# A second split product for pairs of gate tiles, a split product at the start of the first block's down stage, and a fixed bank

## The chip, the cores and the metric

The kernel runs on one core of a Trainium2 chip. TensorE (PE) multiplies matrices into the eight PSUM banks; ScalarE (ACT) and VectorE (DVE) read and write PSUM and SBUF; GpSimd (POOL) works on SBUF alone; SyncE (SP) issues the DMAs. The metric is the device time of one execution in microseconds.

## The reference

The input x is 4 x 2048 tokens of 512 channels, all in fp32. The output is x plus an RWKV-4 attention and a gated feed-forward, both on the same layer norm of x:

```python
xn = layernorm(x)
r, k, v = (mu * xn + (1 - mu) * shifted) @ W.T            # for each of the three, 512 -> 512
attn = (sigmoid(r) * wkv(k, v, w, u)) @ Wo.T
hidden = silu(xn @ W1.T) * (xn @ W3.T)                    # 512 -> 2048
out = x + attn + fwht(hidden) @ W2.T                      # fwht: Hadamard transform, folded into W2
```

`wkv` is a recurrence over time for each channel. In the reference it keeps a running maximum; the kernel computes it with three scans on VectorE and exponentials and relus on ScalarE.

## The kernel before, in words

The tokens are worked on in eight **blocks** of 1024 (two for each batch entry). A block has three parts: the projections k, v and r (six pairs of 128-row tiles), the **up stage** (gate and linear part of the feed-forward, 16 **tiles** `j` = 0 to 15 of 128 hidden units) and the **down stage** (W2 and Wo together, on the 2048 hidden and 512 attention rows). Blocks repeat every 368.6 us in the steady state.

Matrix products are made by the seven-product form of a 2x2 block multiplication. For an up tile (`up_rest`) the four blocks are W1 and W3 over the two halves of the channels; the right side is the normalized input, halves of channels by halves of 512 tokens. Seven combinations of weights, **forms** 0 to 6, are kept in DRAM (`part_w`), and each is multiplied with one combination of the input: form 0 with `b11` (part of `xnT`), form 4 with the first sum `t1` (in `tf`). A form's product is two matmuls of 128x128 weights with 512 columns; in the trace an fp32 matmul leaves two records. Between products ScalarE copies a bank's partial result into another bank, and VectorE adds the stored product of form 4, called `s5`.

Form 0 is already split once more. Two tiles 2p and 2p+1 share their right side, so the form-0 weights of both tiles are again a 2x2 block, and `pair_product` makes seven matmuls with half as many columns (256) where four with 512 would stand. The text calls its steps **P0 to P6** by the number given to `matmul`; they come in the order P1, P0, P2, P4, P5, P3, P6. The pair's weights are made in block 0 by POOL (`make_pair`, `keep_pair`), are kept in `pair_w` and are loaded for each pair from block 1 on. The sums of the right side lie in `pair_sums` (in row 0 of `k_sb`, free by then). The result of a pair lands in `pair_out`, the left half by a ScalarE copy and the right half by a VectorE sum, and `fill` copies it into the banks `pb` and `pa` of each tile. Pairs begin with `FIRST_PAIR` = 2, so tiles 4 to 15 are filled this way: their products are forms 4, 5, 1, 3, 6 and 2, in this order, on the banks pf, pb, pa, pb, pc and pd. The product of pair p is computed beside tile 2p-2, one or two of its steps after each form.

The order on each engine is written out by hand: everything is issued through `InOrder` (line 36 in every row of the profile), and each engine works its queue in that order. `up_pairs` drives a tile as a generator and calls the pair's generator after each of its steps. `step()` issues one of the 40 **pieces** of the recurrence (`wkv`): in blocks from 1 on each of the four rows h has ten pieces, row 0 in the projections and rows 1 to 3 over five tiles each (tiles 1 to 5, 6 to 10, 11 to 15), two pieces per tile. Pieces 9 and 10 are the longest on VectorE (a half reciprocal, the numerator, the two final products); they fall on tiles 5, 10 and 15. Between the pieces VectorE does the gate of each tile: the sums with s5, `h0` and `h1`, and at the start of the next tile the **tail** (tanh of h1 on ScalarE, then h0 times pd, h1 times pc, h1 times pb).

Banks are handed out by `take` and given back by `give`, oldest first, from block 1 on; block 0 rotates with `bank()`. In the down stage the pieces of weights (five tiles of 128x128 each) stream through eight slots of `pieces_w`. Blocks 1 to 7 (`down`) split every form once more (`Deep`): seven steps of five 256-wide matmuls. Block 0 (`down_whole`) has plain products: four pieces of five 512-wide matmuls for each form. `Deep.clear` zeroes half a bank on ScalarE before the first step; `before` issues the tail of tile 15 and what is left of the recurrence. `Chores` spreads the next blocks' statistics and normalizing over the down stage, and `normalize_early` normalizes the block after next during the up stage, through slots in `pieces_w`.

Of the kernel before, what the change touches and what calls it, by code (L numbers as in the profile page):

```python
# [41 lines left out]
def tile_rwkv_attn_hadamard_ffn(  # L42
# [37 lines left out]
    down_w = dram.tile([2, 7, KH, P, QR, P], F32, name="down_w")  # L80
    deep_w = dram.tile([7, 7, P, QR, P], F32, name="deep_w")

    pair_w = dram.tile([NF // 2, P, 7, P], F32, name="pair_w")
    stat_d = dram.tile([n_blocks, 2, TB], F32, name="stat_d")
    xn_d = dram.tile([C, TB], F32, name="xn_d")

# [7 lines left out]
    sa, sb = (const.tile([P, OFF + TB], F32, name=n) for n in ("sa", "sb"))  # L94
    e1b, e1 = (const.tile([P, TB], F32, name=n) for n in ("e1b", "e1"))
    banks = [ps.tile([P, H], F32, name=f"bank{b}") for b in range(8)]
    free_banks = deque(banks)

    NP = NF // 2

# [22 lines left out]
    def take():  # L123
        return free_banks.popleft()
# [6 lines left out]
    tf_flat = tf.rearrange("p f k t -> p (f k t)")  # L131
    x_first, x_tok = (flat.rearrange("p (t c) -> p t c", c=C) for flat in (k_flat, tf_flat))

    pair_sums = k_sb[:, 0, :].rearrange("p (n t) -> p n t", n=4)
    pair_out = v_sb[:, 0, :].rearrange("p (n t) -> p n t", n=2)
    pair_s5 = unit(NF - 1)[:, 0 : H // 2]

    pair_forms = pieces_w[:, 7].rearrange("p q c -> p (q c)")[:, 0 : 4 * P].rearrange("p (f c) -> p f c", f=4)
    spread = v_sb[:, 0:2, :]
    stage = [v_sb[:, 2 + s // 2, ts(s % 2, H)] for s in range(4)]  # L140
    u2_of = [e1b[:, ts(g, H)] for g in range(KH)]
# [80 lines left out]
    def normalize_early(i):  # L222

        flat = pieces_w.rearrange("p u q c -> p (u q c)")
        both = flat[:, 0 : 2 * TB].rearrange("p (s t) -> p s t", t=TB)
        slots = [flat[:, ds((2 + n) * TB, TB)] for n in range(3)]

        def load(b):
            sp.dma_start(out=slots[b % 3], in_=xT[ts(b, P), ds(i * TB, TB)])

        load_spread(i, both)
        for b in range(3):
            load(b)
        yield
        for b in range(NB):
            xb = slots[b % 3]
            for s, op in ((0, ALU.mult), (1, ALU.add)):
                dve.tensor_tensor(xb, xb, both[:, s, :], op)
                if s:
                    sp.dma_start(out=xn_d[ts(b, P), :], in_=xb)  # L240
                    if b + 3 < NB:
                        load(b + 3)
                yield


# [226 lines left out]
    def load_parts(i, chunk):  # L472
        kind, n = chunk
        t = ring_a.tile([P, 7, KH, P], F32, tag="a", name=f"part_{i}_{kind}_{n}")
        if kind == "pair":
            sp.dma_start(out=t.rearrange("p f k c -> p (f k) c")[:, 0:7], in_=pair_w[n])
        elif kind == "rest":
            sp.dma_start(out=t[:, 1:7], in_=part_w[n][:, 1:7])
        elif is_first(i, n):
            sp.dma_start(out=t[:, 0:4], in_=wpart[n])  # L480
            forms_in(t)
        else:
            sp.dma_start(out=t, in_=part_w[n])
        return t

    def make_pair(p, w0, w1):
        (a11, a12), (a21, a22) = ([w[:, 0, b] for b in range(KH)] for w in (w0, w1))
        seven_forms([pair_forms[:, n] for n in range(4)], a11, a12, a22, a21)
        sp.dma_start(out=pair_w[p][:, 0:2], in_=w0[:, 0])
        sp.dma_start(out=pair_w[p][:, 2], in_=w1[:, 0, 1])  # L490

    def keep_pair(p):
        sp.dma_start(out=pair_w[p][:, 3:7], in_=pair_forms)

    def is_first(i, n):
        return i == (1 if n < 3 * KH else 0)
# [59 lines left out]

    def fill(row):

        pb, pa = take(), take()
        act.copy(pb, pair_out[:, row])
        act.copy(pa, pair_out[:, row])
        return pa, pb

    def up_rest(key, j, w, filled, tail, step, then):

        m11, m21, m22, f1, f2, f3, f4 = right_of["up"]
        h0, h1 = unit(j)[:, 0:H], unit(j)[:, H:TB]

        def product(pt, form, right, start=False):
            for b in range(KH):
                pe.matmul(
                    pt, lhsT=w[:, form, b, :], rhs=right[:, b, :], start=start and b == 0, stop=b == KH - 1,
                    skip_group_check=True,
                )

        if filled:
            pa, pb = filled
        else:  # L580
            pa, pb = take(), take()
            product(pa, 0, m11, True)
            act.copy(pb, pa)
        pf = take()
        product(pf, 4, f1, True)
        s5 = small.tile([P, H], F32, tag="s5", name=f"s5_{key}")
        act.copy(s5, pf)
        give(pf)
        yield
        product(pb, 5, f2)  # L590
        pc = take()
        act.copy(pc, pb)
        for f in tail:
            f()
        yield
        product(pa, 1, m21)
        act.activation(h0, pa, AF.Tanh, scale=0.5)
        yield
        product(pb, 3, f3)
        dve.scalar_tensor_tensor(h0, h0, 1.0, pa, ALU.add, ALU.mult)  # L600
        give(pa)
        pd = take()
        act.copy(pd, pb)
        yield
        step()
        dve.tensor_tensor(pb, pb, s5, ALU.add)
        product(pc, 6, m22)
        dve.tensor_tensor(pc, pc, s5, ALU.add)
        yield
        then()  # L610
        step()
        product(pd, 2, f4)
        yield (
            lambda: act.activation(h1, pc, AF.Tanh, scale=0.5),
            lambda: dve.tensor_tensor(h0, h0, pd, ALU.mult),
            lambda: dve.scalar_tensor_tensor(h1, h1, 1.0, pc, ALU.add, ALU.mult),
            lambda: dve.tensor_tensor(h1, h1, pb, ALU.mult),
            lambda: give(pd, pc, pb),
        )

    def pair_quarters():
        return [b11[:, b, cols] for b in range(KH) for cols in (lo, hi)]

    def make_pair_sums():
        q11, q12, q21, q22 = pair_quarters()
        t1, t2, t3, t4 = (pair_sums[:, n] for n in range(4))
        for out, x, y in ((t1, q12, q11), (t2, q22, t1), (t3, q22, q12), (t4, q21, t2)):
            difference(out, x, y)

    def pair_product(w):  # L630

        w = w.rearrange("p f k c -> p (f k) c")
        q11, _, q21, q22 = pair_quarters()
        t1, t2, t3, t4 = (pair_sums[:, n] for n in range(4))
        a, b = take(), take()

        def matmul(n, pt, right, start=False):
            pe.matmul(pt, lhsT=w[:, DEEP_AT[n]], rhs=right, start=start, stop=True, skip_group_check=True)

        def out(row, pt):  # L640
            act.copy(pair_out[:, row, lo], pt[:, lo])
            dve.tensor_tensor(pair_out[:, row, hi], pt[:, hi], pair_s5, ALU.add)


        matmul(1, a[:, hi], t1, True)
        act.copy(pair_s5, a[:, hi])
        yield
        matmul(0, a[:, lo], q11)
        act.copy(b[:, hi], a[:, lo])
# [8 lines left out]
        yield  # L658
        matmul(6, b[:, lo], t4)
        yield  # L660
        out(0, a)
        out(1, b)
        give(a, b)
        yield

# [1 line left out]

    def up_pairs(i, chunk, tail, step, beside):

        filled = None  # L670
        for j in range(1, NF):
            w = chunk(2 if j % 2 and j > 1 else 1)
            beside(j)
            ahead = []

            def fill_next():
                if 2 * FIRST_PAIR <= j + 1 < NF:
                    ahead.append(fill((j + 1) % 2))

            rest = up_rest(f"{i}_{j}", j, w, filled, tail, step, fill_next)  # L680
            product = iter(())
            for n in range(6):
                left = next(rest)
                if n == 0 and j % 2 == 0 and j + 2 < NF:
                    product = pair_product(chunk(0))
                next(product, None)
            tail, filled = left, ahead[0] if ahead else None
        return tail
# [85 lines left out]
        return [("deep", m, n) for n in which]  # L774

    order = (0, 1, 4, 6, 5, 3, 2)
    whole_program = [p for form in order for p in plain(form)]
    program = [p for n in (0, 4, 1, 2, 3, 5) for p in (*deep(6, n), *deep(0, n))]
    program += [*deep(1, 0), *deep(6, 6), *deep(0, 6)]
    for m, *which in (  # L780
# [75 lines left out]
                    self.product(("plain", form, (rh, g)), pts[g], rows, whole, start and rh == 0)  # L856
                then(g)

    def down_whole(i, chores, next_parts):

        d = Down(i)
        y11, y12, y21, y22 = (parts_of(kh, half) for kh in range(2) for half in range(2))
        pa, pb, pc = ([bank() for _ in range(KH)] for _ in range(3))
        s5 = [small.tile([P, H], F32, tag="s5", name=f"s5_{i}_d{g}") for g in range(KH)]
        d.residual(x11, 0, 0)
        d.plain_product(0, pa, (0, 0), lambda g: act.copy(pb[g], pa[g]), True)
        differences(y11, y12, y11)
        chores.start()
        chores.statistics(2 * TP + 1)
        next_parts()  # L870

        def c11(g):
            add(x11[g], pa[g])
            d.store(x11[g], 0, g, 0)

        d.plain_product(1, pa, (1, 0), c11)
        d.residual(x12, 0, 1)
        d.residual(x22, 1, 1)
        d.plain_product(4, pc, (0, 0), lambda g: act.copy(s5[g], pc[g]), True)
# [75 lines left out]
    def down(i, chores, next_parts, last, before):  # L955
# [1 line left out]
        d = Down(i)  # L957
        y11, y12, y21, y22 = (parts_of(kh, half) for kh in range(2) for half in range(2))
        early = list(free_banks)
        late = [pt for pt in banks if not any(pt is b for b in early)]  # L960
        pa, sets = early[0:2], [[early[2], early[4], early[3]], late]

        def slot(flat, n=0):
# [271 lines left out]
    for i in range(n_blocks):  # L1235
# [111 lines left out]


        if i:
            make_pair_sums()  # L1350
            tail = up_pairs(i, chunk, tail, step, lambda j: staging(i, j))
        for j in range(NF if i == 0 else 0):
            if j % 2 and j > 2 * FIRST_PAIR:
# [35 lines left out]
                loaded[0] = 2  # L1389

        if i == 0:
            before()
            down_whole(i, Chores(i + 1), next_parts)
        else:
            down(i, Chores(i + 1), next_parts, last, before)

# [52 lines left out]
```

## Time and profile before

| | us |
|---|---|
| median of 3 runs (3011.78 to 3013.1) | 3012.85 |
| profiled run, device time | 3011.08 |
| its span in the trace | 3009.3 |
| PE busy | 2993.2 |
| DVE busy | 2428.0 |
| ACT busy | 1266.0 |
| down stage of block 0, PE start to the next block's first matmul | 301.71 to 422.12 |
| down stage of block 3, PE start | 1055.80 |

The profile's page gives the busy time of each engine, the chain of work that ended last (followed back from the last instruction to whatever released each step), and the costliest groups of instructions. A row of the timeline gives the start, the length, the engine, the operation with out<-in, the shape and a count, and in brackets the idle time before it and who ended it. Since the kernel has one line for all instructions, rows are told apart by their tiles: `right<-right,bank` on DVE is the gate, `e`, `e1b`, `sa` and `sb` are the recurrence, `bank<-...,part_pair` is a pair's step, `v_sb<-bank` is a pair's output.

By stage, in block 3: between 950 and 1000 us (tiles 6 to 10) DVE is busy 41.49 of 50.00 us and ACT 28.69; between 1035.20 and 1055.80 (tiles 14 and 15) DVE is busy 20.30 of 20.60 us. Between 1066 and 1168 (down stage) DVE is busy 91.09 of 102.00 us. PE is busy in all of these.

### The profile page before, as it was taken

To read this page: it belongs to the slowest core of one execution; us is meant where nothing else is said; L and a number is where in the kernel's file an instruction comes from. 1 tells how busy PE (TensorE), PEld (TensorE's weight loads), DVE (VectorE), ACT (ScalarE), POOL (GpSimd) and SP (SyncE) were. 2 spreads that over 40 slices of the span, in tenths; PEclk is the share of its full clock that TensorE was granted. 3 is DMA by queue.
4 is the path that set the end of the run, shared out by engine and by line. 5 is a ranking of instruction groups with operands and counts; after the bars stand their busy time and mean duration, and the time that the engine had idled before them with its cause. 6 is when DMAs were issued, how large, how long until landed. Compare 5 with 4: busy or idle time off the path is not lost.

```text
span 3009.3 us, 26145 instructions
## 1 busy us (share of the span) xinstructions
PE 2993.2 (99%) x8954; PEld 1699.2 (56%) x8954; DVE 2428.0 (81%) x2637; ACT 1266.0 (42%) x2328; POOL 230.5 (8%) x220
## 2 busy tenths in 40 slices
PE   8999999999999999999999999999999999999999
PEld 3444444448644486445854558545585446844568
DVE  7688547789878897788977889778887788877887
ACT  4334134553345523554235542455425454144441
POOL 4264012220000000000000000000000000000000
PEclk9999999999999999999999999999999999999999
DMA  4266523666423374233633336332463324622244
GB/s 177 90 222 226 220 88 126 225 231 234 139 102 112 110 235 134 103 113 115 231 120 121 106 142 210 116 119 96 158 202 118 121 99 136 203 96 74 92 141 150
DMA packets 154979, 440.22 MB, mean 146 GB/s; under 512 B 16352, under 2 KB 36320, under 8 KB 152672
## 3 DMA queue, kind: packets, MB, share of 16 engines
q1 hardware_dynamic: 154560, 437.97, 42.6%
q8 instruction: 72, 1.18, 0.2%
q10 hardware_dynamic: 288, 0.59, 0.1%
q14 instruction: 59, 0.48, 0.0%
HBM read 363.01 MB, written 75.49 MB: 146 GB/s over the span
## 4 chain that ended last, share of the span: by engine, by line
PE 92%; DVE 7%; ACT 1%; DMA 0%; issue 0%; SPq 0%; DVEq 0%; ACTq 0%
PE bank L36 92%; DVE e1b L36 3%; DVE right L36 2%; DVE bank L36 1%; DVE e L36 1%; DVE v_sb L36 0%; ACT bank L36 0%; DMA xnT<-xT 0%; DVE sa L36 0%; ACT right L36 0%; DVE sb L36 0%; SPq L36 0%; DVE xnT L36 0%; DVE tf L36 0%; DVEq L1445 0%
## 5 line engine op out<-in xcount | busy, mean ns | idle before, releaser
L36 ACT COPY bank<-bank 128x512 f32<-128x512 f32 (+1 forms) x701 | 344.2, 491 | 999.1 <-PE bank L36 956.8
L36 PE MATMUL bank<-right,pieces_w 128*128 128x256 f32 (+1 forms) x2928 | 736.4, 409 | 2.9 <-ACT bank L36 2.9
L36 PEld LDWEIGHTS bank<-right,pieces_w 128*128 128x128 f32 x2928 | 555.1, 190 | 173.1 <-issue 99.2
L36 PE MATMUL bank<-tf,part_rest 128*128 128x512 f32 x1344 | 611.3, 592 | 1.6 <-ACT bank L36 1.6
L36 PEld LDWEIGHTS bank<-tf,part_rest 128*128 128x128 f32 x1344 | 255.1, 190 | 279.3 <-issue 248.3
L36 PE MATMUL bank<-right,part_full 128*128 128x512 f32 x840 | 369.6, 593 | 0.0
L36 DVE SCALAR_TENSOR_TENSOR right<-right,bank 128x512 f32<-128x512 f32 x256 | 175.1, 684 | 240.1 <-ACT right L36 239.4
L36 DVE TENSOR_TENSOR right<-right 128x1280 f32<-128x1280 f32 (+2 forms) x236 | 327.7, 1414 | 13.0 <-PE bank L36 12.0
L36 PE MATMUL bank<-tf,part_full 128*128 128x512 f32 x704 | 324.8, 592 | 0.0
L36 PE MATMUL bank<-xnT,part_rest 128*128 128x512 f32 x672 | 315.8, 592 | 0.0
L36 PEld LDWEIGHTS bank<-right,part_full 128*128 128x128 f32 x840 | 158.4, 190 | 203.2 <-issue 183.9
L36 ACT ACTIVATE right<-bank 128x512 f32<-128x512 f32 x308 | 184.1, 600 | 155.7 <-PE bank L36 110.2
L36 PE MATMUL bank<-xnT,part_full 128*128 128x512 f32 x528 | 248.1, 592 | 0.0
L36 PEld LDWEIGHTS bank<-tf,part_full 128*128 128x128 f32 x704 | 133.8, 190 | 159.4 <-issue 149.7
L36 DVE RECIPROCAL e1b<-e1b 128x512 f32<-128x512 f32 x64 | 213.9, 3343 | 0.0
L36 DVE TENSOR_TENSOR bank<-bank,s 128x512 f32<-128x512 f32 x256 | 168.2, 691 | 42.3 <-PE bank L36 29.8
L36 PEld LDWEIGHTS bank<-xnT,part_rest 128*128 128x128 f32 x672 | 127.7, 190 | 130.9 <-issue 117.2
L36 DVE TENSOR_TENSOR right<-right,bank 128x512 f32<-128x512 f32 x256 | 173.9, 679 | 6.5 <-PE bank L36 2.0
L36 PEld LDWEIGHTS bank<-xnT,part_full 128*128 128x128 f32 x528 | 100.3, 190 | 117.8 <-issue 113.3
L36 ACT COPY s<-bank 128x512 f32<-128x512 f32 x128 | 74.5, 582 | 214.0 <-PE bank L36 213.0
L36 PE MATMUL bank<-k_sb,pieces_w 128*128 128x256 f32 x630 | 146.3, 379 | 0.0
L36 DVE SCALAR_TENSOR_TENSOR right<-xnT,vec,right 128x1024 f32<-128x1024 f32 x92 | 121.9, 1355 | 21.3 <-ACT right L36 21.3
(137 smaller groups left out, 3160.3 us busy)
## 6 DMA issues: line engine op xcount, KB each, us to landing
pieces_w<-deep_w SPq DMA_DIRECT2D x343, 320.0 KB, 3.1
part_rest<-part_w SPq DMA_DIRECT2D x84, 768.0 KB, 4.3
part_full<-part_w SPq DMA_DIRECT2D x64, 896.0 KB, 4.6
part_w<-part_full SPq DMA_DIRECT2D x22, 896.0 KB, 6.7
part_pair<-pair_w SPq DMA_DIRECT2D x42, 448.0 KB, 4.1
pieces_w<-down_w SPq DMA_DIRECT2D x56, 320.0 KB, 4.7
deep_w<-pieces_w SPq DMA_DIRECT2D x7, 2240.0 KB, 8.6
tf<-x SPq DMA_DIRECT2D x7, 2048.0 KB, 7.9
```

The lines of the kernel that those rows point to most:

```text
L36: return self.tc.keep_in_program_order(issue(*args, **kwargs))
```

## The change

Five things are changed.

- **A second split product.** `make_pair` also makes the seven weights of form 4 of both tiles (POOL's sums go through `k_sb` row 0), and `pair_w` keeps two sets. In blocks 2 to 7, `up_pairs` starts a second `pair_product` beside the odd tile 2p-1, with weights loaded into `pair_w1` (a part of `pieces_w`) and right-hand sums made from `t1` at tile 2 (`make_pair_sums(1)`, kept in unit 14). Its two results go straight into the `s5` buffers of tiles 2p and 2p+1. `up_rest` then leaves out its own product of form 4 and the copy of it.
- **Slots.** `normalize_early` has two slots for its rows instead of three, which frees the place of `pair_w1`.
- **Block 0's down stage.** The first form is no longer a plain product but a `Deep` one, and the four plain pieces of form 1 stand between its steps, on banks of their own (`pc`). The tail is issued after the clearing of two banks. The statistics of the next block and the next weights are issued after both forms instead of after the first.
- **Clearing.** `down_whole` now calls `before` itself.
- **The bank.** `down` orders the three banks of its late set so that `pd` of tile 15 (`last_d`) is the one that is cleared after the tail.

```diff
-    pair_s5 = unit(NF - 1)[:, 0 : H // 2]
+    pair_sums = [t.rearrange("p (n t) -> p n t", n=4) for t in (k_sb[:, 0, :], unit(NF - 2))]
+    pair_s5 = [unit(NF - 1)[:, ts(n, H // 2)] for n in range(2)]
+    pair_w1 = pieces_w.rearrange("p u q c -> p (u q c)")[:, ds(4 * TB, 7 * P)].rearrange("p (f c) -> p f c", f=7)
...
     def make_pair(p, w0, w1):
+        for n, form in enumerate((0, 4)):
+            (a11, a12), (a21, a22) = ([w[:, form, b] for b in range(KH)] for w in (w0, w1))
+            seven_forms([pair_forms[n][:, m] for m in range(4)], a11, a12, a22, a21)
+            sp.dma_start(out=pair_w[n, p][:, 0:2], in_=w0[:, form])
+            sp.dma_start(out=pair_w[n, p][:, 2], in_=w1[:, form, 1])
...
-        pf = take()
-        product(pf, 4, f1, True)
-        s5 = small.tile([P, H], F32, tag="s5", name=f"s5_{key}")
-        act.copy(s5, pf)
-        give(pf)
+        if s5 is None:
+            pf = take()
+            product(pf, 4, f1, True)
+            s5 = small.tile([P, H], F32, tag="s5", name=f"s5_{key}")
+            act.copy(s5, pf)
+            give(pf)
...
+        def out(slot, pt):
+            act.copy(slot[:, lo], pt[:, lo])
+            dve.tensor_tensor(slot[:, hi], pt[:, hi], s5, ALU.add)
...
+            both = i >= 2 and pair >= FIRST_PAIR
             for n in range(6):
                 left = next(rest)
+                if n == 0 and pair >= FIRST_PAIR and 2 * pair < NF:
+                    if j % 2 == 0:
+                        product = pair_product(0, chunk(0).rearrange("p f k c -> p (f k) c"), kept)
+                        if both:
+                            sp.dma_start(out=pair_w1, in_=pair_w[1, pair])
+                    elif both:
+                        product = pair_product(1, pair_w1, new_s5)
                 next(product, None)
...
+    whole_program = [
+        *deep(6, 0), p1[0], *deep(6, 4), p1[2], *deep(6, 1, 2), p1[1], *deep(6, 3, 5), p1[3], *deep(6, 6), *whole_program
+    ]
...
+        d6 = Deep(d, 6, (*pa, pb[0]), y11, [*in_k, in_k[1]], s5_first[:, lo])
+        d6.clear()
+        before()
+
+        def beside(g, rh):
+            rows = quarter(1, 0, rh, whole)
+            d.product(("plain", 1, (rh, g)), pc[g], rows, whole, rh == 0)
+
         d.residual(x11, 0, 0)
-        d.plain_product(0, pa, (0, 0), lambda g: act.copy(pb[g], pa[g]), True)
+        d6.step(0)
+        beside(0, 0)
+        d6.step(4)
+        d6.forms(0, 1)
+        beside(1, 0)
+        d6.step(1, 2)
+        d6.forms(2, 3)
+        beside(0, 1)
+        add(x11[0], pc[0])
+        d6.step(3)
         differences(y11, y12, y11)
+        d6.step(5)
         chores.start()
+        beside(1, 1)
+        add(x11[1], pc[1])
+        d6.step(6)
+        for g in range(KH):
+            act.copy(pb[g][:, lo], pa[g][:, lo])
+            dve.tensor_tensor(pb[g][:, hi], pa[g][:, hi], d6.s5, ALU.add)
+            add(x11[g], pb[g])
+            d.store(x11[g], 0, g, 0)
         chores.statistics(2 * TP + 1)
         next_parts()
...
-        late = [pt for pt in banks if not any(pt is b for b in early)]
+        late = [pt for pt in banks if not any(pt is b for b in (*early, last_d[0]))] + last_d
```

## The prediction

> **What bounds the kernel.** I read the page's busy line and clock row first, then the chain of waits, then the timeline of block 3 (one of the six steady blocks), engine by engine.
>
> ```profile
> PE 2993.2 (99%) x8954; PEld 1699.2 (56%) x8954; DVE 2428.0 (81%) x2637; ACT 1266.0 (42%) x2328; POOL 230.5 (8%) x220
> PEclk9999999999999999999999999999999999999999
> PE 92%; DVE 7%; ACT 1%; DMA 0%; issue 0%; SPq 0%; DVEq 0%; ACTq 0%
> ```
>
> TensorE streams nearly all the time at full clock. A busy TensorE can hide slack, so I took start-to-start times: a form's product (two 512-wide matmuls, four records) repeats every 1.72 us, a 256-wide pair step every 0.43 us, a 256-wide piece of five matmuls every 2.16 us, a 512-wide piece every 4.30 us. Half the columns cost half the time: fewer columns is a real gain for TensorE.
>
> But the chain leaves TensorE once in each block, for VectorE, for about 22 us. This is its end in block 3:
>
> ```profile
> 1057.92 1.29 DVE L36 TENSOR_TENSOR bank<-bank,s 128x512 f32<-128x512 f32 x2
> 1059.12 1.22 DVE L36 SCALAR_TENSOR_TENSOR right<-right,e 128x1024 f32<-128x1024 f32 x1
> 1060.37 1.22 DVE L36 SCALAR_TENSOR_TENSOR right<-right,e1b 128x1024 f32<-128x1024 f32 x1
> 1061.51 0.68 DVE L36 TENSOR_TENSOR right<-right,bank 128x512 f32<-128x512 f32 x1
> 1062.23 0.39 ACT L36 ACTIVATE bank<-had_sb 128x256 f32<-128x256 f32 x1 [2.11 <-DVE right L36]
> 1062.55 0.33 ACT L36 COPY bank<-bank 128x256 f32<-128x256 f32 x1
> 1062.93 2.43 PE L36 MATMUL bank<-right,pieces_w 128*128 128x256 f32 x10 [0.33 <-ACT bank L36]
> ```
>
> VectorE finishes the last recurrence pieces and tile 15's h0; ScalarE may then clear a bank and copy; TensorE's fourth down step starts, 0.33 us late. **VectorE and TensorE are level there.** VectorE has run since 1030.98 with less than 0.3 us idle.
>
> **The change on TensorE.** Per pair of tiles two form-4 products go (2 x 1.72) and seven steps come (7 x 0.43): -0.43 us. Six pairs in six blocks (2 to 7): -15.5 us. It is not spread evenly. T(j) is TensorE's start of tile j. Before T(13), nine tiles (4 to 12) lose 1.72 each, 15.44, and five new products (tiles 3, 5, 7, 9, 11) cost 15.02: -0.43. From T(13) on, three tiles lose 5.15 and one product costs 3.00: -2.15, and that is where VectorE ends last.
>
> **From T(13) to the down stage.** Before, T(13) = 1024.91 (form 2 of tile 12 starts at 1023.19 and takes 1.72); VectorE's first op on tile 13's gate starts at 1030.98 (+6.07), since ScalarE's tanh waits for form 1, third in the tile. After, form 1 ends at +4.40 (without form 4, behind two pair steps), tanh starts 0.20 later, VectorE 0.63 after that (distances between such rows elsewhere: TensorE's end to ScalarE's start, 970.55 to 971.18): +5.23. Its queue from there took 31.2 us (1030.98 to 1062.19) and gains the two half-width sums of the new product, 0.67; less small gaps, it ends at +36.99. Clear and copy add 0.74: TensorE resumes at +37.73, before at +38.02. **Only 0.29 of 2.15 us arrives**; the rest is waiting in the first down steps.
>
> **Where the change adds waits.** After it every tile from 4 to 13 carries a pair product. TensorE's order in a tile, with ends from its start: P1 0.43, form 5 2.15, P0 2.58, form 1 4.30, P2 4.73, form 3 6.45, P4 P5 P3 7.73, form 6 9.45, P6 9.88, form 2 11.60. `take` hands out banks oldest first. In tile j, a is pa of tile j-1, b is its a, and **pc is its b**, the bank that VectorE reads last when it writes the pair's second output. Until then ScalarE's copy pb to pc waits, and in its queue behind it stand tanh h1, then the copy into b that P2 adds onto. So a late pair output reaches TensorE. Tile 10 before:
>
> ```profile
> 995.41 3.34 DVE L36 RECIPROCAL e1b<-e1b 128x512 f32<-128x512 f32 x1
> 998.67 1.16 DVE L36 TENSOR_TENSOR e<-e,sa 128x1024 f32<-128x1024 f32 x1
> 999.87 1.22 DVE L36 TENSOR_TENSOR e<-e,v_sb 128x1024 f32<-128x1024 f32 x1
> 1001.01 1.29 DVE L36 TENSOR_TENSOR bank<-bank,s 128x512 f32<-128x512 f32 x2
> 1002.21 1.22 DVE L36 SCALAR_TENSOR_TENSOR right<-right,e 128x1024 f32<-128x1024 f32 x1
> 1003.46 1.23 DVE L36 SCALAR_TENSOR_TENSOR right<-right,e1b 128x1024 f32<-128x1024 f32 x1
> 1004.60 0.75 DVE L36 TENSOR_TENSOR v_sb<-bank,right 128x256 f32<-128x256 f32 x2
> 1005.10 0.57 ACT L36 COPY bank<-bank 128x512 f32<-128x512 f32 x1 [1.32 <-DVE v_sb L36]
> ```
>
> The last two rows are this wait already: T(11) = 1001.28 (form 2 of tile 10 ends), so outputs end at +4.07. It cost nothing, because tile 11 had no pair product.
>
> After, in tile 10: gate op at +5.35, 0.60; reciprocal and numerator 5.60; two adds 1.20; last piece 2.39; outputs 0.75: end +15.89, which is T(11)+4.29. In tile 11: copy to pc 4.34, tanh h1 0.48 later at 4.82, copy into b 0.49 later at 5.31 (steps of such rows) to 5.69, P2 at 5.74 where TensorE was ready at 4.30: **1.44 us**. Tile 5 has the same pieces (one row's work takes five tiles), so tile 6 stalls as much; there odd tiles had no outputs before. In tiles 7 and 12, light in VectorE work, the lag is caught up. At least 1.2 us each if VectorE enters tile 10 without lag; I take 1.44.
>
> **A rule against the change.** The Trainium skill's page "PSUM — Partial Sum Buffer", section "PSUM bank collisions raise a hardware error", says engines must be kept apart by bank, not by address. By addresses P0 (left half of a) needs no wait for the copy of a's right half; by banks it does. The nearest row agrees with banks: VectorE's right-half sum starts when ScalarE's left-half copy ends:
>
> ```profile
> 1026.44 0.76 DVE L36 TENSOR_TENSOR v_sb<-bank,right 128x256 f32<-128x256 f32 x2 [1.66 <-ACT v_sb L36]
> ```
>
> ScalarE comes to that copy late where long activations stand ahead of it. Outputs and copy then end at +2.2 to +2.4, and P0, ready at 2.15, waits 0.32 in tile 4, 0.10 in 8, 0.25 in 9, 0.10 in 13 (already in the +37.73); tiles 5 and 10 lose 0.02 each. By addresses a block's stalls before T(13) are 2.9 us, by banks 3.59. I take banks, and keep 2.9, or 2.4 with the smaller stalls, for the range.
>
> The stalls stay short of the idle window of about 3.4 us after which the page "TensorE: Matmul & The Clock Gate" (Part 1) has the clock halved; no run here shows such a drop, and I count none.
>
> **Block 0's down stage.** Twenty 512-wide matmuls (17.2 us) become 35 of 256 (15.1): -2.1. But the second plain piece of form 1 starts a new bank, pc[1], which is tile 15's pb. VectorE frees it with the tail's last row:
>
> ```profile
> 301.71 120.57 PE L36 MATMUL bank<-right,pieces_w 128*128 128x512 f32 x280
> 311.80 0.69 DVE L36 TENSOR_TENSOR right<-right,bank 128x512 f32<-128x512 f32 x1
> ```
>
> TensorE is there after 2.16 + 4.30 + 2.16, at 310.33, and waits until 312.54: +2.2. Net **+0.1**. Statistics move about 17 us later on ScalarE; their spread then lands near 356, when VectorE's normalizing started anyway (356.20), with 3 us of slack behind it.
>
> **The other bank.** Block 1's down stage waits 0.93 us (694.35) because the bank to clear is pc, freed by the tail's second op; blocks from 2 on have pd. With pd fixed block 1 saves one op, **-0.6**.
>
> **Hidden.** The four sums of the second set (1.5 us of VectorE at tile 2) lie before form 5 ends at 5.6 there. The second pair weights (448 KB; part_pair lands in 4.1 us) are asked for when a tile begins, needed 11.6 later. Two slots instead of three make SP wait for one more store, around tile 7; weights are two chunks ahead. POOL makes four more sums per pair in block 0 (1.9 us), with 2 to 8 us idle per tile. If these covers went, each costs its excess alone.
>
> **Sum.** Per block: -0.43 + 3.59 - 0.29 = +2.87; six blocks +17.2; block 0 +0.1; block 1 -0.6: **+16.7**. Span 3009.3 becomes 3026.0; the profiled run took 3011.08, 1.8 outside the span: **3028 us**. That run is 1.8 below the median of the runs shown, 3012.85. About 6 us (0.2%) is what can be told from no change.
>
> **Rivals.**
> 1. Outputs come in time, no stall (0.13): six blocks gain 0.43 + 0.29, block 1 0.6: -4.8, 3006. For it: VectorE is 81% busy and a 0.86 us earlier gate op per tile helps it. Against: row 1005.10, and 15.1 us of queue in tile 10 after an 11.6 us tile. It holds if the outputs end by +2.85, for then P2 never waits; below 6 us it may count as the same or as faster.
> 2. TensorE keeps all (0.08): 15.5 + 2.1 + 0.6 = 18.2, 2993. For it: 99% busy, 92% of the chain. Against: 31 us of full VectorE queue at each block's end.
> 3. The second pair weights come late (0.07): slower beyond 11.6 us after the issue; 36 loads, 1 us late each, 3064. Against: 4.1 us to landing.
> 4. The forecast (0.72): 3019 to 3036, low for stalls of 2.4 per block and a tail 0.2 better, high for 1.3 more per block.
>
> The range 3004 to 3040 takes in the first rival. Faster: all of 2 and part of 1, 0.13; within 0.2%: the rest of 1 and an edge of 4, 0.11; slower: 0.76.
>
> **What would show it.** In each steady block TensorE gaps before the P2 of tiles 6 and 11, about 1.4 us, released by ScalarE, with ScalarE's copy before them released by VectorE; a gap of some 2 us in the first down steps in place of 0.33; one of 2.2 us near 310; block 1's gap down to 0.33. No gap in tile 11 would refute the stalls; a down stage that starts without a gap would refute the tail.

## The result, and the profile after

The changed kernel takes 3040.81 us (median of 4 runs, 3039.85 to 3041.86); the kernel before takes 3012.85 (median of 3). The ratio is 1.0093, with a 95% interval of 1.0079 to 1.0107: it is slower by 28 us, 0.9%. A fourth execution of the kernel before took 6501.43 us; nothing on record explains it, and it counts neither in the median nor in the ratio. The forecast was 3028, with a range up to 3040. The profiled execution took 3041.11 us, and its span is 3039.1.

The page of the changed kernel, first the busy times with the number of instructions, then the granted clock in 40 slices, then the engines' shares of the chain that ended last:

```profile
PE 2990.0 (98%) x9200; PEld 1743.4 (57%) x9200; DVE 2471.2 (81%) x2741; ACT 1295.0 (43%) x2478; POOL 254.6 (8%) x244
PEclk9999999999999999999999999999999999999999
PE 78%; DVE 18%; ACT 2%; DMA 1%; POOL 1%; issue 0%; SPq 0%; ACTq 0%; DVEq 0%; POOLq 0%
```

VectorE's share of the chain rose from 7 to 18%: TensorE now waits for it more often. The clock row shows nothing, since a drop of a few microseconds disappears in a slice of 76.

**The steady blocks.** One block now takes 371.50 us from down stage to down stage (before: 368.57), so each of six costs 2.93 us more, 17.6 in all. The timeline below is of the block that was called block 3 so far; counted from 0, as block 0 and block 1 are, it is block 2, the first with the second product. It shows the start of tile 11 in the changed kernel (start, length, engine, operation, count, and in brackets the idle time before and who ended it):

```profile
1018.07 1.23 DVE L36 SCALAR_TENSOR_TENSOR right<-right,e1b 128x1024 f32<-128x1024 f32 x1
1019.21 0.75 DVE L36 TENSOR_TENSOR v_sb<-bank,right 128x256 f32<-128x256 f32 x2
...
1020.05 0.57 ACT L36 COPY bank<-bank 128x512 f32<-128x512 f32 x1 [3.23 <-DVE v_sb L36]
1020.53 0.60 ACT L36 ACTIVATE right<-bank 128x512 f32<-128x512 f32 x1
1021.02 0.39 ACT L36 COPY bank<-bank 128x256 f32<-128x256 f32 x1
...
1021.47 0.70 PE L36 MATMUL bank<-right,pieces_w 128*128 128x256 f32 x2 [1.19 <-ACT bank L36]
```

Read it from the bottom: P2 waits for the copy into b, which stands behind tanh of h1 and the copy of pb to pc; that copy waits for VectorE's pair output, and the output stands behind the last recurrence piece of tile 10. T(11) is 1015.81, so P2 starts at +5.66. Tile 6 has the same wait (961.59).

The end of the same block, where the down stage begins:

```profile
1074.47 0.60 ACT L36 ACTIVATE right<-bank 128x512 f32<-128x512 f32 x1 [6.91 <-DVE bank L36]
1074.97 0.38 ACT L36 COPY bank<-bank 128x256 f32<-128x256 f32 x1
...
1075.40 2.43 PE L36 MATMUL bank<-right,pieces_w 128*128 128x256 f32 x10 [1.60 <-ACT bank L36]
...
1077.34 0.68 DVE L36 SCALAR_TENSOR_TENSOR right<-right,bank 128x512 f32<-128x512 f32 x1
1077.45 0.39 ACT L36 ACTIVATE bank<-had_sb 128x256 f32<-128x256 f32 x1 [2.11 <-DVE right L36]
1077.78 0.33 ACT L36 COPY bank<-bank 128x256 f32<-128x256 f32 x1
```

TensorE comes earlier and waits 1.60 us for ScalarE, which has waited for VectorE, then 0.33 once more before the step at 1078.16. That is T(13) (1040.48) + 37.68; before, it was + 38.02.

**Block 0.** Its down stage took 120.41 us before (301.71 to 422.12) and takes 132.61 now (302.32 to 434.93): 12.2 us more where 0.1 was forecast. TensorE's rows with a wait, and the rows of VectorE and of SP's queue that belong to them:

```profile
313.15 6.26 PE L36 MATMUL bank<-right,pieces_w 128*128 128x512 f32 x10 [2.05 <-DVE right L36]
...
352.77 0.38 SPq L36 DMA_DIRECT2D stat_d<-rs  x1
...
357.72 1.17 SPq L36 DMA_DIRECT2D e<-xT  x2
358.99 11.61 SPq L36 DMA_DIRECT2D pieces_w<-down_w  x8
...
369.67 1.93 DVE L36 TENSOR_TENSOR e<-s_d,e 128x512 f32<-128x512 f32 x2 [23.70 <-DMA e<-xT]
...
371.08 6.26 PE L36 MATMUL bank<-right,pieces_w 128*128 128x512 f32 x10 [2.26 <-DMA pieces_w<-down_w]
...
381.63 53.46 PE L36 MATMUL bank<-right,pieces_w 128*128 128x512 f32 x120 [4.30 <-DVE right L36]
```

The first gap was forecast. The second is a piece of down weights that comes late. The third is VectorE: it stood for 23.70 us with the sum of the residual x22 (`e<-xT`) at the head of its queue, and the normalizing and the differences of the next form came late behind it. Both loads are issued by SP after the store of the statistics. Before, there was no gap, and SP issued the two earlier:

```profile
333.00 0.37 SPq L36 DMA_DIRECT2D stat_d<-rs  x1
...
349.03 1.15 SPq L36 DMA_DIRECT2D e<-xT  x2
```

The loss is larger than the three gaps (2.22, 2.42 and 4.46 us start to start). Ten records of 128x512 take 4.3 us at full clock; after the first two gaps they took over 6. Busy time by stretch in the changed kernel, with the granted clock third from the end (then DMA share and GB/s):

```profile
313.15:314.00 0.85, 0.85 (x2) 0.48 (x3) 0.85 (x1) 0.00 (x0) 0.00 (x0) 1.00 0.66 259
314.00:315.00 1.00, 1.00 (x3) 0.53 (x2) 0.96 (x2) 0.00 (x0) 0.00 (x0) 0.72 0.10 38
315.00:316.00 1.00, 1.00 (x2) 0.34 (x1) 1.00 (x2) 0.00 (x0) 0.00 (x0) 0.50 0.03 13
316.00:317.00 1.00, 1.00 (x2) 0.34 (x1) 1.00 (x2) 0.00 (x0) 0.00 (x0) 0.50 0.00 0
...
318.00:319.00 1.00, 1.00 (x4) 0.52 (x3) 0.00 (x0) 0.00 (x0) 0.00 (x0) 1.00 0.00 0
```

1.3 us after TensorE resumes (1.4 and 1.1 after the other two gaps) its clock falls to one half for some 3.4 us, and it counts as busy all the while. After the second gap the mean clock is 0.73 over 371.08 to 377.30, after the third 0.80 over 381.63 to 390.00. (1 - clock) x length is 1.7 us for each of the three drops.

So block 0: -2.1 saved, +9.1 of gaps, +5.1 of clock: 12.1 of the 12.2. With block 1 (-0.5), the steady blocks (+17.6) and a later start of block 0's down stage (+0.6) the sum is 29.9; the spans differ by 29.8.

### The profile page after: what moved, and what is told of

Its sections match the earlier page's. It is cut to its first block, busy times and chain, and to the rows that moved or that the text cites. A ratio compares the mean times of both kernels' runs of the same rounds, so it can differ in the third digit from the quotient of the medians.

```text
span 3039.1 us, 27050 instructions
## 1 busy us (share of the span) xinstructions
PE 2990.0 (98%) x9200; PEld 1743.4 (57%) x9200; DVE 2471.2 (81%) x2741; ACT 1295.0 (43%) x2478; POOL 254.6 (8%) x244
## 4 chain that ended last, share of the span: by engine, by line
PE 78%; DVE 18%; ACT 2%; DMA 1%; POOL 1%; issue 0%; SPq 0%; ACTq 0%; DVEq 0%; POOLq 0%
PE bank L36 78%; DVE e1b L36 6%; DVE right L36 4%; DVE bank L36 2%; DVE e L36 2%; DVE v_sb L36 1%; ACT right L36 1%; ACT bank L36 1%; DVE sa L36 1%; DVE sb L36 0%; DMA e<-xT 0%; DVE s L36 0%; ACT tf L36 0%; POOL pieces_w L36 0%; DVE xnT L36 0%
## 5 line engine op out<-in xcount | busy, mean ns | idle before, releaser
L36 PE MATMUL bank<-right,pieces_w 128*128 128x256 f32 (+1 forms) x3206 | 819.4, 406 | 27.7 <-ACT bank L36 19.1
L36 ACT COPY bank<-bank 128x512 f32<-128x512 f32 (+1 forms) x812 | 384.9, 474 | 1045.0 <-PE bank L36 953.7
L36 PEld LDWEIGHTS bank<-right,pieces_w 128*128 128x128 f32 x3206 | 608.5, 191 | 249.7 <-issue 124.8
L36 PE MATMUL bank<-tf,part_rest 128*128 128x512 f32 x1056 | 491.6, 592 | 1.7 <-ACT bank L36 1.7
L36 PEld LDWEIGHTS bank<-tf,part_rest 128*128 128x128 f32 x1056 | 200.4, 190 | 172.1 <-issue 149.2
L36 PE MATMUL bank<-k_sb,pieces_w 128*128 128x256 f32 x670 | 155.4, 379 | 0.0
L36 PE MATMUL bank<-tf,pieces_w 128*128 128x256 f32 (+1 forms) x490 | 142.2, 409 | 1.0 <-DVE tf L36 1.0
```

What stands on the lines that cost most here:

```text
L36: return self.tc.keep_in_program_order(issue(*args, **kwargs))
```

## Experiments

### Each part alone

Theory: up stages and block 0 are two separate losses. In `up_only`, block 0's down stage and its order of pieces are as before:

```diff
-            down_whole(i, Chores(i + 1), next_parts, before)
+            before()
+            down_whole(i, Chores(i + 1), next_parts)
```

`down_whole` itself and `whole_program`, the order in which the pieces of weights are loaded, are those of the kernel before too. In `down0_only`, only these are changed in the kernel before.

> The changed kernel with block 0's down stage as before; the second split product, the two slots and the fixed bank stay. Theory (each steady block pays about 2.9 us by stalls in tiles 6 and 11, and block 0's down stage pays 12 us by itself): 3012.9 + 6 x 2.9 - 0.6 = about 3030 us, with the stall gaps before the third pair step of tiles 6 and 11 unchanged. Rival (the late loads and stalls of block 0 come from the second product, whose weights are also made and stored in block 0): the down stage of block 0 stays some 12 us longer, about 3041.

> The kernel before with only block 0's down stage and its piece order changed. Theory: the 12 us are this edit's own, 3012.9 + 12 = about 3025 us, with TensorE gaps of about 2.2, 2.3 and 4.3 us in block 0's down stage. Rival (they need the second product's stores and POOL work beside them): below 3016.

Measured: `up_only` 3030.75 us (ratio 1.0061, 1.0046 to 1.0076), with no wait and full clock in block 0's down stage. `down0_only` 3024.17 (1.0038, 1.0023 to 1.0053), whose timeline has the three gaps again, with the same releasers:

```profile
313.07 6.25 PE L36 MATMUL bank<-right,pieces_w 128*128 128x512 f32 x10 [2.05 <-DVE right L36]
...
371.38 6.25 PE L36 MATMUL bank<-right,pieces_w 128*128 128x512 f32 x10 [2.63 <-DMA pieces_w<-down_w]
...
381.89 53.46 PE L36 MATMUL bank<-right,pieces_w 128*128 128x512 f32 x120 [4.26 <-DVE right L36]
```

17.8 and 11.2 us make 29.0, for 28.0 of both together: the losses add. The up part alone (with block 1) was forecast at 17.2 - 0.6 = 16.6.

### What holds block 0: the residual ahead of the statistics

In `resid_first`, the changed kernel issues two loads earlier, and nothing else:

```diff
+        d.residual(x12, 0, 1)
+        d.residual(x22, 1, 1)
         chores.statistics(2 * TP + 1)
         next_parts()
         s5 = [small.tile([P, H], F32, tag="s5", name=f"s5_{i}_d{g}") for g in range(KH)]
-        d.residual(x12, 0, 1)
-        d.residual(x22, 1, 1)
```

> The changed kernel with the residuals x12 and x22 of block 0 issued ahead of the statistics in SP's queue. Theory (x22 is stuck behind the store of the statistics and the large loads after it, VectorE waits 23.7 us for it and then cannot make the differences in time): the 4.3 us gap near 381 goes, with it the low clock after it, -5 to -6, so about 3035 us; the 2.3 us gap for late down weights may stay. Rival (the spread of the statistics is what comes late): the gap stays, about 3041.

Measured: 3030.48 us (1.0058, 1.0043 to 1.0073), 10.3 less than the changed kernel, about twice what I had expected. The gap near 381 is gone, the one near 371 as well, and with them the drops of the clock. The order on SP's queue is shown as the cause of the late residual; that the late weights went too I had not foreseen: their first issue after the statistics came at 355.11 instead of 358.99. Only the first gap stays, and in this kernel full clock follows it:

```profile
313.62 4.56 PE L36 MATMUL bank<-right,pieces_w 128*128 128x512 f32 x10 [2.05 <-DVE right L36]
...
351.56 0.38 SPq L36 DMA_DIRECT2D stat_d<-rs  x1
...
357.88 7.27 DVE L36 TENSOR_TENSOR xnT<-xnT,v_sb 128x1024 f32<-128x1024 f32 x6 [1.81 <-DMA v_sb<-stat_d]
```

The last two rows clear the statistics themselves: they are stored nearly as late as in the changed kernel (351.56 instead of 352.77), and VectorE's normalizing waits for their spread. It starts at 357.88, 1.7 us later than in the kernel before, and no gap of TensorE follows.

### The bank of the first gap

`bank_swap` is `resid_first` with one more line, so that the second plain piece starts a bank that tile 15's tail frees early:

```diff
         pa, pb, pc = ([bank() for _ in range(KH)] for _ in range(3))
+        pb[1], pc[1] = pc[1], pb[1]
```

> The changed kernel with the residual loads of block 0 ahead of the statistics (3030.48 us), and in block 0's down stage the two banks pb[1] and pc[1] exchanged, so that the second plain piece starts a bank that tile 15's tail frees early. Theory: the wait of 2.05 us near 313 us is for that bank alone; it goes and nothing takes its place: 3030.5 - 2.1 = 3028.4 us (3027 to 3030). Rival: the wait moves to the next user of the same bank or to tail data (y11 or the hidden rows of tile 15): no gain, 3030 to 3032.

Measured: 3026.99 us (1.0047, 1.0033 to 1.0061). TensorE's rows have no bracket left there; forty 256-wide records include the place of the gap:

```profile
302.34 13.06 PE L36 MATMUL bank<-right,pieces_w 128*128 128x256 f32 x40
315.24 4.48 PE L36 MATMUL bank<-k_sb,pieces_w 128*128 128x256 f32 x20
```

Block 0's down stage with block 1 up to its own now takes 383.0 us (302.34 to 685.34); before 384.9, changed 397.2. The split saves its 2 us here once nothing waits. The medians differ by 3.5 us from `resid_first`, the spans of the profiled executions by 2.5, where the gap accounts for 2.1; what the rest is, no row shows.

### The P2 waits: outputs ahead of the piece

Theory: the pair's outputs come late because they are issued behind the tile's last recurrence piece. `outs_first` issues them ahead of it in every tile, in `fill_next`, which `up_rest` calls just before `step()`:

```diff
                 if 2 * FIRST_PAIR <= j + 1 < NF:
                     ahead.append(fill((j + 1) % 2))
+                next(product, None)
...
-                next(product, None)
+                if n < 5:
+                    next(product, None)
```

> The changed kernel with a pair's two outputs issued before the last recurrence piece of their tile instead of after it. Theory (late outputs hold the bank that the next tile copies into, and ScalarE's queue passes that on to TensorE): outputs end near 1.9 instead of 4.2 us into the next tile, the two gaps of about 1.35 us per block and most small ones go, 6 x 2.9 = about -17, so about 3023 us. Rival (VectorE has too much work in these tiles, whatever its order): the gaps move by a tile and the time stays within 4 us of 3041.

Measured: 3050.59 us (1.0124, 1.0107 to 1.0141): a miss, 10 us slower than the changed kernel. The waits of tiles 6 and 11 did go, but tile 4 shows what came instead (timeline of `outs_first`):

```profile
930.74 2.13 ACT L36 ACTIVATE e<-e 128x1024 f32<-128x1024 f32 x2
...
931.80 0.68 DVE L36 TENSOR_TENSOR right<-right,bank 128x512 f32<-128x512 f32 x1
932.78 0.35 ACT L36 COPY right<-bank 128x256 f32<-128x256 f32 x1
...
933.18 0.70 PE L36 MATMUL bank<-xnT,part_pair 128*128 128x256 f32 x2 [2.01 <-ACT right L36]
```

The last piece of tile 3 is piece 6, with some 4 us of exponentials on ScalarE. The outputs' copies now stand ahead of them in ScalarE's queue, and the second copy waits there for 1.97 us, until VectorE has summed the first output; so the exponentials start late and hold the next copy that P0 needs. Tiles 9 (0.99 us) and 14 (0.67) have such waits too, and the first down step waits 2.40.

So the order should change only where the last piece leaves ScalarE alone: piece 10, in tiles 5 and 10. That is `outs_p10`:

```diff
+                if j % 5 == 0:
+                    next(product, None)
...
-                next(product, None)
+                if n < 5 or not (j % 5 == 0):
+                    next(product, None)
```

> The changed kernel, with a pair's two outputs issued ahead of the recurrence piece of that step in tiles 5 and 10 alone (whose last piece is piece 10, all on VectorE). Theory: the P2 waits of tiles 6 and 11 come from the place of the outputs behind that piece, and the miss of the version with outputs first in every tile came from tiles 3, 8, 13 (piece 6 keeps ScalarE for some 4 us). Then both waits of about 1.2 to 1.4 us go, nothing takes their place: about 2.7 us for each of six blocks, 16 in all, 3024 us (3021 to 3029). Rival A: VectorE has too much to do in these tiles whatever the order; the wait then appears in another place of tiles 5 to 7 or at the block's end (the first down steps wait 1.6 + 0.33 us now, then about 4.5): 3038 to 3042. Rival B: the outputs ahead of the piece hold ScalarE there too, slower: 3045 to 3052.

Measured: 3023.18 us (1.0034, 1.0021 to 1.0047), 17.6 less than the changed kernel; the block takes 368.61 instead of 371.50. In its timeline, at the end of tile 5, the second output (now an s5 of the next pair) stands ahead of the two long rows of piece 10, and tile 6's P2 at 959.86 has no bracket:

```profile
957.16 0.42 DVE L36 TENSOR_TENSOR s<-bank,right 128x256 f32<-128x256 f32 x1 [0.17 <-ACT s L36]
957.50 1.22 DVE L36 SCALAR_TENSOR_TENSOR right<-right,e 128x1024 f32<-128x1024 f32 x1
958.75 1.23 DVE L36 SCALAR_TENSOR_TENSOR right<-right,e1b 128x1024 f32<-128x1024 f32 x1
...
959.86 0.59 PE L36 MATMUL bank<-k_sb,part_pair 128*128 128x256 f32 x2
```

The wait was the place of two small operations in VectorE's queue, not the amount of VectorE's work.

### The end of the block: two pieces earlier

`two_hooks` issues two more recurrence pieces in the projections, so that pieces 9 and 10 fall on tiles 4, 9 and 14 and tile 15 has none:

```diff
-                    if hooks[0] in (5, 6, 8, 10, 11, 12, 13, 14, 15, 17):
+                    if hooks[0] in (5, 6, 8, 10, 11, 12, 13, 14, 15, 16, 17, 18):
```

> The changed kernel with two more recurrence pieces issued in the projections of each block from 1 on, so that every later piece moves one tile forward (pieces 9 and 10 on tiles 4, 9, 14; none on tile 15). Theory: the 1.60 + 0.33 us that the first down steps wait in each block are VectorE's queue since T(13), some 31 us full; with pieces 9 and 10 one tile earlier VectorE ends earlier by several us, the down waits go, and the waits of about 1.4 us at the P2 of tiles 6 and 11 move to tiles 5 and 10: about 2 us per block less for six or seven blocks, 3027 us (3024 to 3032). Rival: the projections have no room on VectorE; the steps wait there or delay the first tiles: 3038 to 3050.

Measured: 3027.12 us (1.0047, 1.0033 to 1.0061), a block in 369.05. The waits at the down stage are gone, and the P2 waits moved one tile forward, as the theory has it:

```profile
948.25 0.75 DVE L36 TENSOR_TENSOR v_sb<-bank,right 128x256 f32<-128x256 f32 x2
...
950.50 0.70 PE L36 MATMUL bank<-right,pieces_w 128*128 128x256 f32 x2 [1.20 <-ACT bank L36]
```

### All four, and what is the change's own part

`combined` has the two pieces earlier, the outputs ahead in tiles 4, 9 and 14 (`j % 5 == 4`), the exchanged bank and the early residual.

> All four edits together: two more pieces in the projections, outputs ahead of the piece in tiles 4, 9 and 14 (where pieces 9 and 10 then lie), the exchanged bank and the early residual loads in block 0. Theory: if all causes are independent and as told, each steady block keeps the 2.58 us that TensorE saves (368.57 - 2.58 = 366.0) and block 0 its 2.08, block 1 its 0.6 or more: 3012.9 - 15.5 - 2.1 - 0.6 - about 0.3 for block 1's down wait = 2994 us, with some small P0 waits 2994 to 3000; faster than the kernel before by about 0.5 %. Rival: VectorE's load is the bound however it is arranged (76 to 80 % busy over the block, but full in places), and a new wait of 1 to 3 us per block comes: 3002 to 3018.

Measured: 2994.62 us (0.9939, 0.9926 to 0.9951): 0.6% faster than the kernel before, and 46 us faster than the change as it came. A block takes 366.13 us; after the first 19 us TensorE's rows have one bracket in all, of 1.57 us in block 1. Its page has the busy times and the chain:

```profile
PE 2978.7 (100%) x9200; PEld 1744.3 (58%) x9200; DVE 2475.2 (83%) x2741; ACT 1298.3 (43%) x2478; POOL 256.6 (9%) x244
...
PE 98%; DVE 1%; DMA 0%; ACT 0%; issue 0%; ACTq 0%; DVEq 0%
```

Is this the split's gain or the order's? `before_sched` gives the kernel before the two edits of order, with no part of the change; `up_sched` is `combined` with block 0's down stage as before.

> The kernel before, without the change, with the same two edits of order as the best version (two more recurrence pieces in the projections; a pair's outputs ahead of the last piece in tiles 4 and 9, where it has any). Theory: the edits only remove waits; before has 0.33 us of them in each of the blocks 2 to 7 and 0.93 us in block 1, so it gains 3 us at most: 3009 to 3012 us, and the rest of the best version's gain belongs to the split products. Rival: the order itself is worth much, whatever is split: 2995 to 3004.

> The best version (2994.62 us) with block 0's down stage and its order of pieces as in the kernel before. Theory: freed of its waits, block 0's split is worth the 2.08 us that TensorE saves there, no more and no less: 2996.7 us (2995.5 to 2998.5). Rival: it is worth nothing (its sums and copies cost elsewhere what it saves): 2993.5 to 2995.5.

Measured: `before_sched` 3006.1 us (0.9977, 0.9968 to 0.9986), `up_sched` 2996.71 (0.9945, 0.9933 to 0.9958). `up_sched` is as expected: block 0's split is worth 2.1 us by the medians (its down stage takes 118.1 us in the trace of `combined`, 120.4 in that of `up_sched`). The gain of `before_sched`, 7 us, is over twice what I had expected. The block went from 368.57 to 367.82, by 0.75, where I had counted the 0.33 in the bracket. Start to start, the two steps around that bracket in the kernel before are late by 0.66 and 0.11 us: a record outlasts the spacing of its group (ten 256-wide records are spaced 2.16 us and shown with 2.32), so a bracket understates a wait. Six times 0.75, with 1.35 in the block from block 1's down stage on, are 5.9 of the 7.

So of the 18 us by which `combined` beats the kernel before, some 7 are the order's alone and some 11 (3006.1 to 2994.62) the change's, with block 0's loads and bank put right.

## Why the prediction missed

**Right: the gain on TensorE and where it is lost.** 2.58 us less per block stood in the forecast. `combined` against `before_sched` gets 1.69 of it, most of the rest going into eight delays of about 0.1 us each in the tiles, too short for a bracket. The two slots of `normalize_early` were not tried alone; what these delays leave for them is 0.1 us per block.

**Right: the P2 waits.** Forecast 1.44 us each, P2 at T(11)+5.74; measured +5.66, and 1.36 us start to start with 0.11 behind it. With small delays start to start (0.2 in tiles 4 and 9, 0.1 in 5, 8 and 10) the losses before T(13) are 3.6 us; forecast 3.59 by banks, 2.9 by addresses. `outs_p10` shows the cause of the P2 waits.

**Right: the tail.** Forecast T(13)+37.73, measured +37.68; `two_hooks` shows that VectorE's queue, not the first down steps, set it. A block: forecast +2.87, measured +2.93. (That the chain of the kernel before leaves TensorE once in each block holds for blocks 2 to 7, which the forecast is about; in block 1 it does so several times between 551 and 694 us.)

**Right: block 1 and the first gap.** Forecast -0.6 and +2.2, measured -0.5 and +2.22; `bank_swap` shows that it is the bank alone.

**Wrong: the rest of block 0.** The step that failed is "Statistics move about 17 us later on ScalarE; their spread then lands near 356, when VectorE's normalizing started anyway (356.20), with 3 us of slack behind it". I followed the spread and not the queue that issues it. Behind the statistics' store, which waits for ScalarE, SP's queue also holds the residual x22 and the down weights; they came late, and VectorE, which meets x22's sum before the normalizing, stood. `resid_first` shows it: 10.3 us come back for two loads moved ahead. There the normalizing still starts 1.7 us late for the spread and costs nothing, so the slack that I counted on was there.

**Wrong: the clock.** "The stalls stay short of the idle window of about 3.4 us after which the page 'TensorE: Matmul & The Clock Gate' (Part 1) has the clock halved; no run here shows such a drop, and I count none" holds for the steady blocks (waits of 1.2 to 1.6 us, clock 1.00). It does not hold for block 0, where gaps of 2.05 and 2.26 us were enough. About 5 of the 12 us are this. What that page of the Trainium skill has right is the half rate and the length of the slow time (3.4 us here); that 3.4 us of idle time are needed, these traces do not show (last section).

In spans, 3026.0 were forecast and 3039.1 measured. Gaps of 6.9 us that I had not counted, 5.1 of clock, 0.4 in the steady blocks and the 0.6 by which block 0's down stage starts later are 13.0 of these 13.1. The 3028 itself stands on the profiled run, which is 1.8 us below the median; on the median the same sum would have given 3029.6.

## What to carry to other kernels

When an instruction is moved later, list everything that stands behind its DMA on the issuing queue, not only who uses its result: a store that waits for an engine holds every load behind it. A wait at TensorE may come from where two small operations stand in another engine's queue; before giving up a split, move them ahead of the long operation, but only where this leaves the third engine's long work alone. Judge such waits by start-to-start times, since the idle time in a row leaves out part of them.

## What the runs showed of the hardware

The clock dropped to one half after gaps much shorter than I expected, and not each time. The same gap of 2.05 us near 313 was followed by some 3.4 us at half clock in four kernels (the changed one, `down0_only`, `outs_p10`, `two_hooks`: ten records in 6.25 us) and by full clock in two (`outs_first`, `resid_first`: 4.56 us). In `outs_first` a gap of 2.01 us in tile 4 was also followed by a drop (clock 0.57 over 3 us). The Trainium skill's page "TensorE: Matmul & The Clock Gate" (Part 1) says that the window in which activity is counted runs freely, so that its phase against the kernel differs from run to run.

The traces agree: the drops lie on a regular grid. The stretches shown above already give the start of one, since a mean clock of 0.72 between 314 and 315 means half clock from 314.44 on. Finer stretches give 314.45, 372.47 and 382.71 for the three drops of the changed kernel, and 314.34, 372.36 and 382.60 in `down0_only`. In both kernels they are 58.02 and 10.24 us apart, 17 and 3 times 3.413 us, although the gaps before them are not equally far apart (the first two end 57.9 us apart in one kernel and 58.3 in the other). The drops of `outs_p10`, `two_hooks` and `outs_first` lie on grids of this step too, and so does the drop at the end of each of these traces.

Call one step of the grid a window. In the four kernels with a drop near 314 the gap lies inside one window (changed kernel: window 311.03 to 314.45, gap 311.09 to 313.15), and the half clock begins where that window ends. In the two that were spared, the edge of a window cuts the gap: at 312.92 in `outs_first` (gap 311.74 to 313.79) and at 312.21 in `resid_first` (gap 311.56 to 313.62; its grid is counted back from the drop at its end, 3025.81).

How much idle time is enough can be estimated from the starts of TensorE's records in the twelve traces. Among the windows that have matmuls behind them, all 17 drops follow one with at least 2.12 us of idle time out of 3.41; no window with less was followed by a drop, and a single one with more (2.13 us) was not. So what counts here is the idle time that falls into one window, and a gap of some 2 us costs a drop or not by where the edge lies. None of the gaps of 1.2 to 1.6 us read here was followed by a drop. No run set the phase on purpose.
